# Attention weights transposed by the DMA crossbar instead of TensorE, with all v products moved into the attention stretch

## The chip, the cores and the metric

The kernel runs on one core of one Trainium2 chip. The metric is the device time of one execution in microseconds (us), less is better. Each run below is the median of its executions on one chip, beside executions of the kernel before on the same chip.

The kernel keeps its tiles in two memories: those that TensorE writes in pools of PSUM (`ps_1` and `ps_2` below), those of the pools `work` and `group` in SBUF. In the traces TensorE multiplies, VectorE, ScalarE and GpSimd do the rest of the arithmetic, and SyncE only issues DMAs, as GpSimd also does.

A second number goes through the whole text: the **period**. The kernel works on 128 batches in 32 groups of four, and in the middle each group repeats the one before. I take the start of the first TensorE product number 5 (the second q/k product) of each group from the trace, and average its distance from group to group over groups 2 to 29. One microsecond of period is about 31 us of the time.

## The reference, cut to what matters

```python
# layer 0: x is 128 batches of 128 x 512, fp32
x = layernorm(x + relu(max_over_the_512_columns(adj @ x) + b))
# layer 1: attention with 8 heads, masked by adj, then a projection and a norm
q, k, v = x @ w_qkv
attn = softmax(mask(q @ k.T * scale))          # 8 x 128 x 128 per batch
o = (attn @ v) @ w_proj + b_proj
x = layernorm(x + o + layernorm(o) * ln_gamma + ln_beta)
```

The attention product in both kernels reads `attn` transposed (`pav<-eT,v` in the traces, 2048 times for 128 batches), so the kernel needs eight transposed 128x128 blocks of fp32 per batch.

## The kernel before

Every engine works through a list of its own, in a fixed order that is set by "places" (numbers in a table, roughly microseconds after a TensorE step). An engine that waits at one entry of its list is late at the later ones, too. The dense products are done in split precision: each operand is split in a high, a low and a correction part (`h`, `l`, `d`), which VectorE and ScalarE prepare.

```python
work = ctx.enter_context(tc.tile_pool(name="work", bufs=2))
...
ps_1 = ctx.enter_context(tc.tile_pool(name="ps_1", bufs=4, space=bass.MemoryType.PSUM))
ps_2 = ctx.enter_context(tc.tile_pool(name="ps_2", bufs=2, space=bass.MemoryType.PSUM))
...
def transpose_e(b):                       # TensorE: eight transposes of a batch
    e, _ = es.pop(b)
    ppts[b] = ps_2.tile([P, H, P], FP, tag="ps2", name=f"ppt_{b}")
    for j in range(H):
        nc.tensor.transpose(ppts[b][:, j, :], e[:, j, :], ident)

def weights_T(b):                         # ScalarE: out of PSUM
    eTs[b] = work.tile([P, H, P], FP, tag="eT", bufs=2, name=f"eT_{b}")
    nc.scalar.copy(eTs[b], ppts.pop(b))
...
def residual_o(b):                        # GpSimd issues an accumulating DMA
    if b < B - G:
        nc.gpsimd.dma_start(xbs[b], os[b], accum_op=ALU.add)
...
def norm_1(b):                            # VectorE
    o, s, xb = os[b], sums_of.pop((b, 1)), xbs.pop(b)
    ...
    nc.vector.scalar_tensor_tensor(
        o, o, s[:, 2:3], gamma_sb, op0=ALU.add, op1=ALU.mult,
    )
    add_sum(b, 2, o, s[:, 1:2], xb)
...
# the order of TensorE in the attention stretch
'pair_order': [('T', 0), ('x', 1), ('T', 1), ('x', 0), ('S', 0), ('S', 1), ('AV', 0), ('AV', 1),
               ('dense', 2), ('po', 0), ('dense', 3), ('po', 1), ('T', 2), ('x', 3), ('T', 3), ('x', 2),
               ('S', 2), ('S', 3), ('AV', 2), ('AV', 3)],
```

In these lists `S` are the scores of a batch, `T` the transposes of its weights, `AV` the attention product, `x` the transposes of the layer-0 result, `conv` the graph product (tile `pa`), `dense` 0 to 3 the v products, `dense` 4 to 11 the q/k products, and `po` the projection.

## Time and profile before

| | before |
|---|---|
| time, median of 3 runs | 2041.28 us (2040.32 to 2041.9) |
| period | 61.92 us |
| TensorE idle between 60 and 2000 us | 12.8 us in all |
| VectorE, ScalarE busy | 81%, 71% |
| moved by DMA | 240.67 MB |

The table reads as follows. Of TensorE's 12.8 us of idle, 9.2 are two waits at the ends of the stretch; from 100 to 1980 us it is 3.6 us in all. So TensorE's own list is the length of a period. VectorE and ScalarE have 19% and 29% of their time free. The prediction shows the lines.

### The profile page before, as it was taken

What the parts mean: (1) busy time and instruction counts of PE and PEld (TensorE: products, weight loads), DVE (VectorE), ACT (ScalarE), POOL (GpSimd) and SP (SyncE); (2) the same over time, 40 slices, a digit from 0 to 9 for tenths busy, and PEclk for the clock granted to TensorE, in tenths of its full rate; (3) what the DMA queues carried; (4) which work ended last, traced back from release to release, by engine and by line L of the source; (5) the groups of instructions that cost most, each with busy time, mean ns of one, the idle gap of its engine ahead of it and who ended that gap; (6) DMA issues with size and microseconds to landing.
All of it is one profiled execution on the core that took longest, in us unless ns stands there. A gap on an engine that the chain in (4) does not pass through costs nothing. (4 is left out here: it accounts for less than half of the span.)

```text
span 2038.5 us, 35386 instructions
## 1 busy us (share of the span) xinstructions
PE 1995.0 (98%) x12033; PEld 1601.2 (79%) x12033; DVE 1652.2 (81%) x2615; ACT 1455.4 (71%) x4130; POOL 694.2 (34%) x1484
## 2 busy tenths in 40 slices
PE   7999999999999999999999999999999999999995
PEld 4688877888887888887888778888878887778874
DVE  7788777987778887778887779877788877798877
ACT  6676867776877767777768677667777677777665
POOL 1132434323334323343223343233343243432234
PEclk8999999999999999999999999999999999999998
DMA  4455455655455545555554545454455544455443
GB/s 151 88 119 119 118 125 106 130 114 129 115 119 110 130 120 124 120 111 123 121 123 115 127 106 130 112 130 117 117 112 128 121 121 123 106 124 124 104 104 88
DMA packets 134437, 240.67 MB, mean 118 GB/s; under 512 B 14704, under 2 KB 18928, under 8 KB 134256
## 3 DMA queue, kind: packets, MB, share of 16 engines
q1 hardware_dynamic: 97680, 172.27, 28.4%
q0 software_dynamic: 36288, 66.08, 22.1%
q8 instruction: 95, 1.56, 0.3%
q14 instruction: 86, 0.70, 0.1%
q10 hardware_dynamic: 288, 0.07, 0.0%
HBM read 138.74 MB, written 100.66 MB: 117 GB/s over the span
## 5 line engine op out<-in xcount | busy, mean ns | idle before, releaser
L333 ACT ACTIVATE e<-e,nmax 128x128 f32<-128x128 f32 x1024 | 396.8, 390 | 183.9 <-DVE nmax L326 183.9
L400 POOL DMA_DIRECT2D xb<-o x124 | 132.8, 1071 | 479.2 <-DVE o L405 449.3
L417 POOL TENSOR_SCALAR sum<-sum 128x1 f32<-128x1 f32 (+1 forms) x322 | 63.5, 197 | 433.5 <-ACT square L411 422.9
L418 POOL TENSOR_TENSOR sum<-sum,mhalf 128x1 f32<-128x1 f32 (+1 forms) x322 | 200.7, 623 | 26.8
L411 ACT ACTIVATE square<-o,sum 128x512 bf16<-128x512 f32 x256 | 183.2, 716 | 15.5 <-DVE o L405 13.1
L333 ACT ACTIVATION_READ_ACCUMULATOR e<-e,nmax 128x1 f32 x1024 | 192.4, 188 | 0.0
L423 POOL TENSOR_SCALAR sum<-sum 128x1 f32<-128x1 f32 x256 | 89.7, 350 | 281.4 <-DVE o L405 280.8
L432 DVE SCALAR_TENSOR_TENSOR o<-o,sum,gamma_sb 128x512 f32<-128x512 f32 x128 | 95.6, 747 | 88.7 <-DMA xb<-o 41.9
L342 DVE TENSOR_TENSOR e<-e,sums 128x1024 f32<-128x1024 f32 x128 | 156.8, 1225 | 4.4
L318 DVE SCALAR_TENSOR_TENSOR e<-psc,mask 128x1024 f32<-128x1024 f32 x128 | 155.5, 1216 | 2.3 <-PE psc L311 2.3
L326 DVE TENSOR_REDUCE nmax<-e 128x8 f32<-128x1024 f32 x128 | 155.2, 1212 | 0.1
L217 POOL DMA_DIRECT2D x<-in_L_gnn_ln_beta_dram x128 | 140.3, 1196 | 10.3 <-issue 10.3
L352 ACT COPY eT<-ppt 128x1024 f32<-128x1024 f32 x128 | 124.9, 1001 | 17.4 <-PE ppt L348 17.4
L348 PE MATMUL ppt<-ident,e 128*128 128x128 f32 x1024 | 132.3, 273 | 0.5 <-DVE qkT L300 0.5
L311 PE MATMUL psc<-qkT 64*128 64x128 f32 x2048 | 131.9, 279 | 0.0
L174 PE MATMUL pa<-xt,adjT 128*128 128x512 f32 x256 | 126.8, 619 | 5.1 <-DMA xt<-in_x_dram 4.7
L311 PEld LDWEIGHTS psc<-qkT 64*128 64x128 f32 x2048 | 119.4, 188 | 11.0 <-issue 5.5
L361 PE MATMUL pav<-eT,v 128*64 128x128 f32 x2048 | 126.4, 276 | 1.2 <-ACT eT L352 1.2
L348 PEld LDWEIGHTS ppt<-ident,e 128*128 128x128 f32 x1024 | 117.6, 141 | 9.5 <-DVE qkT L300 0.8
L190 ACT ACTIVATE xt<-xt,rm 128x512 f32<-128x512 f32 x128 | 91.4, 715 | 37.7 <-POOL rm L184 37.7
L361 PEld LDWEIGHTS pav<-eT,v 128*64 128x64 f32 x2048 | 110.4, 137 | 9.7 <-ACT eT L352 2.2
L440 ACT ACTIVATE o<-o,sum 128x512 f32<-128x512 f32 x128 | 103.0, 806 | 16.5 <-POOL sum L426 16.5
(4778 smaller groups left out, 5615.5 us busy)
## 6 DMA issues: line engine op xcount, KB each, us to landing
xt<-in_x_dram SPq DMA_DIRECT2D x128, 256.0 KB, 2.8
x<-xt SPq DMA_DIRECT2D x128, 256.0 KB, 2.1
x<-in_L_gnn_ln_beta_dram POOLq DMA_DIRECT2D x128, 256.0 KB, 8.6
xb<-x SPq DMA_DIRECT2D x128, 256.0 KB, 3.0
o<-in_L_gnn_b_proj_dram SPq DMA_DIRECT2D x128, 256.0 KB, 4.8
out_dram<-o SPq DMA_DIRECT2D x128, 256.0 KB, 2.0
xb<-o POOLq DMA_DIRECT2D x124, 256.0 KB, 4.2
wraw<-in_L_gnn_w_qkv_dram SPq DMA_DIRECT2D x12, 256.0 KB, 3.2
```

The source lines that it names most:

```text
L174: nc.tensor.matmul(pa[b], adjT, xs[b], start=True, stop=True)
L217: nc.gpsimd.dma_start(x1s[b], row(ln_beta), accum_op=ALU.add)
L311: nc.tensor.matmul(psc[:, s, hp, :], qkT[hs, hp, i, :], qkT[hs, KC + hp, i, :], start=True, stop=True,)
L318: nc.vector.scalar_tensor_tensor(e, pscs.pop(b).rearrange("p s a m -> p (s a) m"), scale, mask_b, op0=ALU.mult, op1=ALU.add,)
L326: nc.vector.tensor_reduce(nmax, es[b], AX.X, ALU.max, negate=True)
L333: nc.scalar.activation(e[:, j, :], e[:, j, :], AF.Exp, bias=nmax[:, j : j + 1], accum_out=sums[:, j : j + 1],)
L342: nc.vector.tensor_tensor(e, e, sums[:, :, None].to_broadcast([P, H, P]), op=ALU.mult)
L348: nc.tensor.transpose(ppts[b][:, j, :], e[:, j, :], ident)
L361: nc.tensor.matmul(pavs[b][s * HD : (s + 1) * HD, hp, :], v[:, h * HD : (h + 1) * HD], eT[:, s * HP + hp, :], start=True, stop=True,)
L400: nc.gpsimd.dma_start(xbs[b], os[b], accum_op=ALU.add)
L411: nc.scalar.activation(square, x, AF.Square, bias=s[:, 0:1], scale=-float(D), accum_out=s[:, 1:2],)
L418: nc.gpsimd.tensor_tensor(s, s, mhalf[:, :n], op=ALU.pow)
```

## The change

The intent is to relieve the engine that is full. ScalarE separates each fp32 weight into its two 16-bit halves, a DMA stores these two planes to DRAM, and a crossbar load (`DMA_TRANSPOSE` in the traces) brings them back transposed, half by half, so that the fp32 words stand together again. TensorE loses 8 transposes a batch. The bias of the projection becomes a constant in SBUF, which saves one load a batch; `o` and `v` have fewer buffers than before (3 instead of 4, 4 instead of 6). All places were set anew, and all four v products moved into the attention stretch, with two of the four projections and two of the four graph products.

```diff
+    def halves(b):
+        e, _ = es.pop(b)
+        planes = work.tile([P, 2, H * P], U16, tag="planes", bufs=1, name=f"planes_{b}")
+        nc.scalar.copy(
+            planes, e.rearrange("p h m -> p (h m)").bitcast(U16).rearrange("p (m s) -> p s m", s=2),
+        )
+        rows[b] = dram.tile([P, 2, H * P], U16, tag="rows", bufs=8, name=f"rows_{b}")
+        nc.sync.dma_start(rows[b], planes)
+
+    def crossbar_T(b):
+        eTs[b] = work.tile([P, H, P], FP, tag="eT", bufs=2, name=f"eT_{b}")
+        nc.sync.dma_start_transpose(
+            eTs[b].rearrange("p h n -> p (h n)").bitcast(U16).rearrange("p (h r) -> p h r", h=H),
+            rows.pop(b).rearrange("n s m -> (n s) m"),
+        )
...
-                vs[g, j] = group.tile([P, D], FP, tag="v", bufs=6, name=f"v_{g}_{j}")
+                vs[g, j] = group.tile([P, D], FP, tag="v", bufs=4, name=f"v_{g}_{j}")
...
-            os[b], pps["o", b][0], 1.0 + 1.0 / HALF, os[b], op0=ALU.mult, op1=ALU.add,
+            os[b], pps["o", b][0], 1.0 + 1.0 / HALF, bias_sb, op0=ALU.mult, op1=ALU.add,
...
-         'beta': [25.0, 24.85, 24.59, 24.66],
+ 'beta': [4.57, 2.09, 14.96, 45.33],
...
+ 'pair_order': [('S', 0), ('S', 1), ('AV', 0), ('AV', 1), ('dense', 0), ('po', 0), ('dense', 1),
+                ('po', 1), ('S', 2), ('AV', 2), ('x', 0), ('S', 3), ('AV', 3), ('x', 1),
+                ('dense', 2), ('dense', 3), ('x', 2), ('x', 3), ('conv', 0), ('po', 2), ('conv', 1),
+                ('po', 3)],
...
+ 'softmax': {'cross': [-14.48, -14.68, -13.71, -6.73],
...
+             'halves': [5.82, 2.29, 0.68, 4.53],
```

The row `beta` sets when GpSimd issues the accumulating DMAs that add `ln_beta` to the stored layer-0 rows.

## The prediction

> **What bounds the kernel now.** I read the page's busy shares first, then the slices, then one repeating stretch of the middle by windows, then the order of time on TensorE and VectorE inside it. The page's list of waits comes last, since it only means something once the bound is known.
>
> ```profile
> span 2038.5 us, 35386 instructions
> ## 1 busy us (share of the span) xinstructions
> PE 1995.0 (98%) x12033; PEld 1601.2 (79%) x12033; DVE 1652.2 (81%) x2615; ACT 1455.4 (71%) x4130; POOL 694.2 (34%) x1484
> ...
> PE   7999999999999999999999999999999999999995
> ...
> PEclk8999999999999999999999999999999999999998
> ```
>
> TensorE is full in all slices but the ends, at full granted clock. The busy share by itself would not prove it (matmuls overlap in the record), so I looked at two windows of 62 us:
>
> ```profile
> core 0: us, PE busy (x) PEld busy (x) DVE busy (x) ACT busy (x) POOL busy (x), PEclk, DMA share, GB/s
> ...
> 738.00:800.00 62.00, 62.00 (x378) 49.90 (x377) 50.73 (x81) 45.04 (x129) 21.53 (x46) 1.00 0.52 119
> 800.00:862.00 62.00, 62.00 (x378) 49.93 (x377) 50.73 (x81) 45.05 (x130) 21.54 (x46) 1.00 0.53 120
> ```
>
> No microsecond without a matmul in flight, VectorE at 50.7 and ScalarE at 45.0 of 62. So the middle is a queue of TensorE work, and a group of four batches costs what its TensorE work costs. The order of time on TensorE gives the period and the slots:
>
> ```profile
> 745.00 1.04 PE L348 MATMUL ppt<-ident,e 128*128 128x128 f32 x8
> 745.87 0.60 PE L224 MATMUL ptx<-ident,xt 128*128 128x128 f32 x4
> ...
> 751.60 1.99 PE L174 MATMUL pa<-xt,adjT 128*128 128x512 f32 x4
> 753.01 0.80 PE L261 MATMUL pp_('o', 42)_7670<-p_h,oh 128*128 128x512 f32 x1
> 753.65 0.39 PE L262 MATMUL pp_('o', 42)_7670<-p_l,ol 128*128 128x512 f32 x1
> ...
> 806.88 1.04 PE L348 MATMUL ppt<-ident,e 128*128 128x128 f32 x8
> ```
>
> Columns: start, length, engine, line, operation. The same place one group later is 806.88 - 745.00 = 61.88 us on, the period. Eight transposes of the attention weights of one batch hold the engine from 745.00 to 745.87: a slot of 0.87 us. The graph product pa is followed by a product whose first matmul holds the engine for 0.64 us (753.01 to 753.65) where its neighbours take about 0.23: leaving pa for a product costs 0.4 us, and before pays it twice a group, since the four pa come in pairs.
>
> [...] This trace has 273 ns from start to end, but eight of them start 109 ns apart (0.87/8), so the slot counts, not the latency. [...] One of the new transfers is 256 x 1024 halves of 2 bytes, 512 KB[...]. Nothing in the trace before decides that, as it has no such transfer. [...]
>
> **The change, part by part.** For 124 of 128 batches:
>
> *Removed from TensorE*: 8 transposes, 0.87 us a batch, 3.48 a group. Over the 31 groups it applies to that is 108 us, the most it can give: 2041 - 108 = 1933.
>
> *Added to TensorE*: the new order separates the four pa from each other (conv 0, projection 2, conv 1, projection 3; conv 2, product 7, conv 3). Four switches instead of two: +0.8 us a group. And all four v products move out of the dense stretch into the attention stretch, so the scores of the next group come directly behind the last q/k product. The last two of their eight head products wait for the VectorE addition to that q/k tile. In the trace before, the addition to v starts 0.27 us after the next TensorE work (789.26 against 788.99) and takes 0.69, so the wait ends about 1.0 us after the product; the first six heads cover 0.75 of it. +0.27 us a group.
>
> *ScalarE*: the copy of the transposed weights out of PSUM goes (1001 ns for 1024 columns), and the copy that separates the halves comes, over 2048 elements a partition. From 616 ns (512 columns) to 1001 (1024) it is 0.75 ns a column, so 1001 + 1024 x 0.75 = 1.77 us, some 0.8 us more than before: +3.1 a group, 45.0 becomes 48.1 of about 60, or 80%. Not the bound.
>
> *VectorE*: the same instructions, 50.7 us in a group that now is about 60 instead of 62; 85%. It is uneven, and that matters: in the attention stretch the new order puts before the head split of the last batch (starts to starts in the trace: 1.14 masking, 1.13 row maximum, 1.37 weights, 0.60 for 512-wide additions and differences, 1.33 for the first two steps of a split, 1.40 for a projection's pair, 1.53 for a first norm) 3 maskings, 2 maxima, 2 weights, 8 splits, 6 differences, 2 projections, 4 v additions, 1 norm: 3.42 + 2.26 + 2.74 + 10.64 + 3.60 + 2.80 + 2.40 + 1.53 = 29.4 us. It starts when the first scores are out (1.5 us) and I count 1.2 us of waits for TensorE in it, so the split is there at about 32.1. TensorE's own work to that point: 4 scores 4.0 (two take 1.98), 4 attention products 3.8, 4 x transposes 1.9, 7 products of 2.80, pa twice with one switch 1.8, the 0.27 above and 0.2 for small switches: 31.6. So about 0.5 us of TensorE idle a group, in front of the fourth projection.
>
> *DMA*: a 512 KB store and a 512 KB crossbar load more each batch, a 256 KB bias load less. The hardware queue moved 172.27 MB at 28.4% of the span, so about 300 GB/s when busy: 1.75 us for the store[...], 0.9 less for the bias, per 15 us: share 0.52 becomes 0.7. The weights of a group are stored a whole stretch before they are used; only the third and fourth crossbar loads wait for a buffer of two, free after the first two attention products. The fourth comes in the SyncE order behind the output store of the previous group's last batch, which I place at 10.5 us after the scores, with its use at 18.8: 8 us of room. A streaming crossbar[...] is hidden; the change's own placing keeps at least 3 us.
>
> *Sum*: 61.88 - 3.48 + 0.8 + 0.27 + 0.5 = 60.0 us a group, 1.9 saved, times 31 = 59: 2041 - 59 = 1982. The tail and start change little (the last four batches still transpose on TensorE). I take 1980.
>
> **Rivals.** (1) *The order fits better than my count*: no wait at the fourth projection and for the scores, 59.2 a group, 1958. For it: all the places were set anew, surely to shut such gaps. Against: the VectorE sum above has almost no slack. (2) *VectorE becomes the bound of the attention stretch*, with 1 to 2 us more than I count, because norms wait for accumulating DMAs as they do now:
>
> ```profile
> L432 DVE SCALAR_TENSOR_TENSOR o<-o,sum,gamma_sb 128x512 f32<-128x512 f32 x128 | 95.6, 747 | 88.7 <-DMA xb<-o 41.9
> ...
> xb<-o POOLq DMA_DIRECT2D x124, 256.0 KB, 4.2
> ```
>
> That idle costs nothing today, as VectorE catches up in the dense stretch. With one norm in the middle of the attention stretch and busier DMA engines it would go straight to TensorE: 61 to 62 a group, 2010 to 2040, the same. (3) *The crossbar goes block by block*[...]: the fourth attention product waits[...] in each group, and SyncE, which issues in order, holds up loads behind it: 2100 to 2350. Against: [...]the short distances chosen. (4) *The single buffer of the halves holds up ScalarE*: the second copy must wait for the 512 KB store of the first (256 KB stores land in 2.0 to 2.1 us, so 3 to 4). I count about 2 us of ScalarE idle there once a group, and 1 to 2 us of room before the v addition behind it feels it. If it did not fit, another 0.5 to 1 us a group: about 2000.
>
> **Range and chances.** 1980, with rival 1 as the good end (1940 if the ends gain too) and rival 2 as the bad one (2030). The 2% line is 2000.5, only 0.65 us a group away from my count, hence 0.68 faster; 0.25 same; 0.07 slower for the crossbar.
>
> **What would show it.** The period in the order of time: 60.0, with the transposes gone and ScalarE's copy of halves at about 1.8 us. TensorE idle, or stretched first matmuls, at the scores (0.3) and at the fourth projection (0.5), released by VectorE or by ScalarE's cast behind it. VectorE over 83% busy. The crossbar load landing in under 8 us and no idle of the attention products for it. Wrong would be: attention products waiting for a DMA (rival 3), VectorE waiting for the accumulated residual within the attention stretch (rival 2), or a period below 59.2, which would mean that the switch of pa or the waits are cheaper than they look here.

The 273 ns are those of one transpose, from the trace before; what that trace does not decide is how long a crossbar load takes. The sum came to 60.0 us a group and 1980 us, in which the crossbar load has no term because it was taken to be hidden. The DMA share of 0.7 counts a time for the load (the store and the bias alone make it 0.58: 0.85 us more in 15). That "a streaming crossbar", one without pauses between its blocks, is hidden, and the 2100 to 2350 us of rival 3, were assumptions and not shown.

## The result, and the profile after

| | before | after |
|---|---|---|
| time, median of 4 runs beside each other | 2041.59 us | 2157.08 us (2149.46 to 2161.51) |
| ratio | | 1.0562 (1.0531 to 1.0594) |
| period | 61.92 us | 65.71 us |
| TensorE idle, 60 to 2000 us | 12.8 us | 151.6 us |
| TensorE below full clock, 60 to 2000 us | 11.9 us | 133 us |

The changed kernel is right and 5.6% slower. The last row adds up the records of a granted clock below full speed.

The head of the page of the changed kernel, with TensorE's busy share and its slices:

```profile
span 2159.7 us, 33692 instructions
...
PE 1967.0 (91%) x11041; PEld 1528.7 (71%) x11041; DVE 1665.0 (77%) x2615; ACT 1548.3 (72%) x4130; POOL 694.7 (32%) x1484
...
PE   7889999889999999989999999999999999899996
```

TensorE has 992 instructions fewer, and is no longer full. The same two windows that the prediction read say it more sharply:

```profile
core 0: us, PE busy (x) PEld busy (x) DVE busy (x) ACT busy (x) POOL busy (x), PEclk, DMA share, GB/s
738.00:800.00 62.00, 59.04 (x325) 46.20 (x325) 47.74 (x75) 44.82 (x124) 20.25 (x44) 0.97 0.73 160
800.00:862.00 62.00, 58.55 (x313) 45.46 (x312) 48.46 (x77) 44.73 (x121) 22.67 (x46) 0.97 0.71 165
```

Where it was 62.00 of 62 us, TensorE is now busy 59, its clock is granted at 0.97, VectorE does less per microsecond and not more, and the DMA share went from 0.52 to 0.73. The list of waits (engine, line, what ended the wait; us in total, times, longest) names them:

```profile
ACT planes L351 <- DMA rows<-planes: 146.9, 30, 9.1
...
PE pav L382 <- DMA eT<-rows: 94.4, 32, 5.5
...
DVE o L450 <- DMA xb<-o: 47.3, 45, 6.2
```

Once a group the attention product waits for its crossbar load, once a group ScalarE waits for the store of the planes before it may fill their only buffer again, and VectorE waits for the accumulated residual. The list of DMA issues (size, median us from issue to landing) puts the store at 3.2 us and the crossbar load at 6.1:

```profile
rows<-planes SPq DMA_DIRECT2D x124, 512.0 KB, 3.2
...
eT<-rows SPq DMA_TRANSPOSE x124, 6.1
```

The first three crossbar loads of a group keep SyncE for 2.6, 2.2 and 2.6 us in the median, the fourth for 7.7. One such place in the order of time, first on TensorE (start, length, engine, line, operation; in brackets the idle time before it and what ended it):

```profile
930.56 1.16 PE L314 MATMUL psc<-qkT 64*128 64x128 f32 x16
936.65 1.97 PE L382 MATMUL pav<-eT,v 128*64 128x128 f32 x16 [4.93 <-DMA eT<-rows]
938.55 1.12 PE L227 MATMUL ptx<-ident,xt 128*128 128x128 f32 x4
```

The same place on SyncE and on GpSimd:

```profile
917.16 2.41 SPq L360 DMA_TRANSPOSE eT<-rows  x1
...
924.52 8.55 SPq L360 DMA_TRANSPOSE eT<-rows  x1
```

```profile
918.68 1.81 POOL L220 DMA_DIRECT2D x<-in_L_gnn_ln_beta_dram  x2 [9.15 <-DMA x<-xt]
920.67 0.81 POOL L220 DMA_DIRECT2D x<-in_L_gnn_ln_beta_dram  x1 [0.18 <-issue]
```

GpSimd issues three `ln_beta` loads at 918.68 to 921.5, since two of them waited for a store and came out together with the next. They are accumulating DMAs: from 922 to 928 the 16 DMA engines are nearly full of their packets, and the last ends at 931.8 (40 to 74 begin each microsecond, 284 to 391 ns each in the mean). The fourth crossbar load is issued at 924.52, in the midst of it; the trace has no packet of it before 928. Most of its packets of 929 to 932 take 18 ns as usual, but a few take up to 3.9 us, so that the mean of a microsecond is 58 to 194 ns. Its last packet ends at 934.6, 10.1 us after the issue, where the packets of two loads of the same size in a quiet stretch, from 906.1 to 910.5, needed 4.5 us together. It is not alone in this: between 922.1 and 926.9 SyncE's queue moves no data at all, and the output store and the residual load that SyncE issued just before, at 922.55 and 923.06, land after 10.0 and 10.1 us, where 2.7 and 2.9 are the medians. And the wait has a second price, which the windows show (same columns as above):

```profile
934.00:936.00 2.00, 0.00 (x0) 0.00 (x0) 1.74 (x3) 0.00 (x0) 1.21 (x2) 0.66 1.08 326
936.00:940.00 4.00, 3.35 (x22) 2.92 (x23) 0.24 (x1) 0.00 (x0) 0.00 (x0) 0.50 0.97 261
940.00:942.00 2.00, 2.00 (x7) 1.59 (x6) 1.85 (x4) 1.70 (x1) 0.00 (x0) 0.64 0.45 137
```

During these 4.93 us without work TensorE's clock is halved (the record begins at 934.6) and stays so until about 941: the attention product has a slot of 1.90 us (936.65 to 938.55) and not 0.95. In this trace half clock goes with waits, but no one length of a wait decides it. From 60 to 2000 us the changed kernel has 26 records of half clock, each with one wait of 1.9 us or more; nine of these waits are shorter than 3 us (1.93 to 2.96). Four waits of 1.6 to 1.8 us and one of 3.42 us cost no clock. The profile page's digits of the clock in its slices still read 9 all through the middle, so the loss has to be looked for in narrow windows.

The loss can be written as a sum. The period before was 61.92; without the transposes 58.44; +0.8 for two more switches of pa, as predicted, and +0.26 for the scores, as measured (a pair takes 2.24 us instead of 1.98): 59.5. In the stretch of 60 to 2000 us there are 29.5 periods of after and 31.3 of before. Idle: 151.6/29.5 - 12.8/31.3 = 4.7. Half clock loses half of its time (1.90 us for the slot of 0.95 above), and only what does not lie in the idle already counted: 109.5 of the 133 us, and 9.1 of the 11.9 before, so (109.5/29.5 - 9.1/31.3)/2 = 1.7. Together 65.9 against a measured 65.7; so the parts are good to some tenths, and nothing large is missing.

### The profile page after: what moved, and what is told of

Its sections match the earlier page's. It is cut to its first block, busy times and chain, and to the rows that moved or that the text cites. A ratio compares the mean times of both kernels' runs of the same rounds, so it can differ in the third digit from the quotient of the medians.

```text
span 2159.7 us, 33692 instructions
## 1 busy us (share of the span) xinstructions
PE 1967.0 (91%) x11041; PEld 1528.7 (71%) x11041; DVE 1665.0 (77%) x2615; ACT 1548.3 (72%) x4130; POOL 694.7 (32%) x1484
## 5 line engine op out<-in xcount | busy, mean ns | idle before, releaser
L351 ACT COPY planes<-e 128x2048 uint16<-128x2048 uint16 x124 | 234.7, 1892 | 152.7 <-DMA rows<-planes 146.9
L382 PE MATMUL pav<-eT,v 128*64 128x128 f32 x2048 | 147.4, 296 | 97.0 <-DMA eT<-rows 94.4
L220 POOL DMA_DIRECT2D x<-in_L_gnn_ln_beta_dram x128 | 113.7, 988 | 322.0 <-DMA x<-xt 309.0
L382 PEld LDWEIGHTS pav<-eT,v 128*64 128x64 f32 x2048 | 121.3, 147 | 111.2 <-DMA eT<-rows 94.2
L441 POOL TENSOR_SCALAR sum<-sum 128x1 f32<-128x1 f32 x256 | 129.7, 507 | 213.0 <-DVE o L423 213.0
L177 PE MATMUL pa<-xt,adjT 128*128 128x512 f32 x256 | 137.7, 625 | 30.1 <-issue 28.1
L235 DVE TENSOR_SCALAR xh<-ptx 128x512 int32<-128x512 int32 x128 | 87.7, 685 | 97.7 <-PE ptx L227 97.3
L329 DVE TENSOR_REDUCE nmax<-e 128x8 f32<-128x1024 f32 x128 | 155.1, 1211 | 0.1
L314 PE MATMUL psc<-qkT 64*128 64x128 f32 x2048 | 148.9, 286 | 0.0
L227 PE MATMUL ptx<-ident,xt 128*128 128x128 f32 x512 | 89.7, 313 | 25.3 <-ACT xt L212 16.8
L423 DVE SCALAR_TENSOR_TENSOR o<-o,sum,xb 128x512 f32<-128x512 f32 x128 | 96.2, 752 | 15.0 <-POOL sum L436 0.9
```

Of the source, the lines that this page charges most:

```text
L177: nc.tensor.matmul(pa[b], adjT, xs[b], start=True, stop=True)
L314: nc.tensor.matmul(psc[:, s, hp, :], qkT[hs, hp, i, :], qkT[hs, KC + hp, i, :], start=True, stop=True,)
L329: nc.vector.tensor_reduce(nmax, es[b], AX.X, ALU.max, negate=True)
L351: nc.scalar.copy(planes, e.rearrange("p h m -> p (h m)").bitcast(U16).rearrange("p (m s) -> p s m", s=2),)
L382: nc.tensor.matmul(pavs[b][s * HD : (s + 1) * HD, hp, :], v[:, h * HD : (h + 1) * HD], eT[:, s * HP + hp, :], start=True, stop=True,)
L441: nc.gpsimd.tensor_scalar(s[:, 2:3], s[:, 0:1], -1.0 / D, None, op0=ALU.mult)
```

## The experiments

At first I held **theory A**: the fourth crossbar load meets the three `ln_beta` loads, and this one wait with its half clock is the loss. The rival, **theory B**: the new order has several chains of almost equal length, and to free one only lets the next come out.

### The collision, two ways

Issue the fourth crossbar load earlier, right behind the third:

```diff
- 'softmax': {'cross': [-14.48, -14.68, -13.71, -6.73],
+ 'softmax': {'cross': [-14.48, -14.68, -13.71, -14.5],
```

This run, and the ones further down that move the second copy of planes, also hold each load behind the store of its own planes, so that it cannot come before it.

> Only the fourth crossbar load of each group moves: in the SyncE order it stands directly behind the third instead of behind the output store and the residual load. Theory A (the load waits in the DMA engines behind three accumulating loads of ln_beta, the idle of TensorE of 2.9 us a group is that wait, and the half clock that follows an idle costs about 2 us more): issue of the fourth load falls from 7.7 us to 2 to 3 us, the attention product no longer waits, half clock after the start is nearly gone, the period falls from 65.7 to 60 to 61 us, the time to 1980 to 2015 us. Rival B (VectorE is the bound of the new attention stretch and the wait for the load only hides it): the idle moves to another instruction, period 63 or more, time above 2075.

Measured: 2169.29 us, ratio 1.0624 (1.0596 to 1.0652), period 65.84. The fourth load still keeps SyncE 7.5 us in the median: third and fourth now go out together, the `ln_beta` loads come out at the same time, and they collide as before. The run missed its aim and decides nothing.

Put the `ln_beta` loads back to the places that they had before:

```diff
- 'beta': [4.57, 2.09, 14.96, 45.33],
+ 'beta': [25.0, 24.85, 24.59, 24.66],
```

> Only the four places of the accumulating loads of ln_beta go back to those of the kernel before, 25 us behind the norm, which takes them away from the fourth crossbar load. Theory A (collision with the accumulating loads): the fourth crossbar load is issued in under 3.5 us and lands in under 7, wait of the attention product under 0.5 us a group, time 1985 to 2020 us. Rival C (the fourth load is late because of its place in the SyncE order, whatever else is in flight): its issue begins at the same place, 12 us after the scores, it lands after 17 to 18 with the use at 18, so no large change from this run would be left to C only if its landing stays at 10 us or more: then time above 2120.

Measured: 2175.65 us, ratio 1.0654 (1.0638 to 1.067), period 66.57. The collision is gone completely: the fourth load keeps SyncE 2.3 us from the same place in its order (so the place alone, rival C of the expectation, was not the cause), there is no idle at all in front of attention products from 60 to 2000 us, and the time below full clock falls from 133 to 68 us. Yet the kernel is not faster. The waits of this run:

```profile
DVE o L450 <- DMA xb<-o: 112.2, 77, 3.8
ACT planes L351 <- DMA rows<-planes: 111.5, 29, 6.4
...
PEld ptx L227 <- ACT v L299: 63.4, 30, 3.4
```

And two lines of its order of time show how one wait becomes another on the way to TensorE:

```profile
1062.37 1.90 ACT L351 COPY planes<-e 128x2048 uint16<-128x2048 uint16 x1 [3.72 <-DMA rows<-planes]
```

```profile
1066.52 0.65 PE L227 MATMUL ptx<-ident,xt 128*128 128x128 f32 x4 [1.83 <-ACT v L299]
```

ScalarE stands 3.72 us in front of its second copy of planes; the copy of a v product stands behind it in ScalarE's list, and the transposes on TensorE need the PSUM buffer that this copy frees. A second chain is longer still. TensorE's largest wait in this run is at the first q/k product of a group, for VectorE's `x_d`: 74.8 us in 28 places from 60 to 2000 us, against 12.3 in the changed kernel. In 27 of the 28 VectorE had stood, less than 6 us earlier, at a norm that waited for its accumulated residual; the `ln_beta` loads are now in flight beside 90 of the 124 accumulating DMAs of the residual (31 in the changed kernel), and these land after 6.7 us in the median beside them, after 3.4 without. One such place:

```profile
1012.88 0.75 DVE L450 SCALAR_TENSOR_TENSOR o<-o,sum,gamma_sb 128x512 f32<-128x512 f32 x1 [2.02 <-DMA xb<-o]
...
1015.16 1.19 PE L272 MATMUL pp_(15, 4)_9309<-x_d,w_d 128*128 128x512 f32 x4 [1.94 <-DVE x_d L241]
```

So the collision is real, but theory A as the one cause has fallen.

Move the fourth attention product to a later place on TensorE, so that it has more room:

```diff
-                ('po', 1), ('S', 2), ('AV', 2), ('x', 0), ('S', 3), ('AV', 3), ('x', 1),
-                ('dense', 2), ('dense', 3), ('x', 2), ('x', 3), ('conv', 0), ('po', 2), ('conv', 1),
+                ('po', 1), ('S', 2), ('AV', 2), ('x', 0), ('S', 3), ('x', 1),
+                ('dense', 2), ('AV', 3), ('dense', 3), ('x', 2), ('x', 3), ('conv', 0), ('po', 2), ('conv', 1),
```

> The fourth attention product is moved behind the third v product on TensorE (2.8 us of useful work before the wait), its load and its head split keep their places in the other orders. The load still lands 10 us or more after its issue, so the wait falls from 2.9 us a group to about 0.5. If an idle[...] costs half clock afterwards (theory A), that cost of about 2 us a group goes too: gain 4 to 4.5 us a group, time 2015 to 2050. If the clock cost were not a result of the idle: gain 2.4 us a group, time 2075 to 2095. Rival B (VectorE bound): gain under 1 us a group, above 2120, as the head split behind this product comes later.

Measured: 2132.33 us, ratio 1.044 (1.0404 to 1.0475), period 64.65. Idle at attention products falls from 90 to 13 us, but idle in front of the x transposes, which wait for ScalarE's v copies, rises from 17 to 68 us. This is the pattern of theory B again: 77 us freed, 51 of them given back in the next place.

### How much is the order, how much the traffic

Four runs take out parts of the traffic; all give wrong results. First, all of it: ScalarE still copies the planes, but they are neither stored nor loaded, and the attention product reads a constant.

```diff
-        nc.sync.dma_start(rows[b], planes)
...
-        nc.sync.dma_start_transpose(...)
+        eTs[b] = eT_fixed
```

> Wrong result on purpose: the halves are copied by ScalarE as in the changed kernel but neither stored nor loaded back; the attention products read one constant tile. All other work keeps its order and places. If the loss is all DMA traffic and the waits for it (theory D), what is left is the count of the prediction: period 59.5 to 61, no half clock, time 1970 to 2010. If the new order itself is worse than counted, with VectorE and ScalarE late in the attention stretch whatever the transfers do (rival B): period 63 or more, time above 2075.

Measured: 2040.54 us (2 runs), ratio 0.9996 (0.9976 to 1.0016), period 61.58. This was the most telling run: **with the transposes gone from TensorE and no traffic at all in their place, the new order is just as long as the old one.** The 3.48 us a group that were taken off TensorE are lost within the order itself. The largest loss, 49.5 us in 29 places (1.7 us each), is in front of the first pa:

```profile
1129.26 1.04 PE L227 MATMUL ptx<-ident,xt 128*128 128x128 f32 x8
1132.24 2.02 PE L177 MATMUL pa<-xt,adjT 128*128 128x512 f32 x2 [1.94 <-issue]
```

```profile
1131.45 0.69 DVE L237 TENSOR_TENSOR x_l<-ptx,xh 128x512 fp32r<-128x512 f32 x1
```

The releaser is given as "issue", which says that the profile saw no semaphore for it. The time tells: VectorE's last reading of an x transpose ends at 1132.14, and pa starts at 1132.24; in all 29 places the distance is 0.10 us. These tiles share the four PSUM buffers of `ps_1`, so pa waits for VectorE to empty one.

Then the store alone (the load replaced by the constant):

> Wrong result on purpose: the 512 KB stores run, the crossbar loads do not (constant tile instead). Theory D with two separate holders: the second copy of halves still waits for the store of the first through the one buffer, shorter since SyncE is not held by a crossbar issue (2 to 3 us instead of 4.7 a group), and costs TensorE 1 to 2 us a group: period 61 to 62.5, time 2010 to 2060. If the stores are harmless: as without traffic. If the stores are the larger part: above 2090.

Measured: 2079.38 us (2 runs), ratio 1.0186 (1.0149 to 1.0222), period 63.12.

The load alone (the first eight batches' planes are read again and again, nothing stored later):

> Wrong result on purpose: only the first eight batches store their halves, later crossbar loads read those eight again, so the loads run with nothing to wait for but their buffer. The accumulating loads of ln_beta are where the change put them. Theory D: the fourth load is still issued in 7 to 8 us behind them and the attention product still waits about 3 us a group with half clock after it: period 63.5 to 65, time 2080 to 2130. If the stores or the wait of the copies cause most of the loss: under 2040.

Measured: 2190.94 us (2 runs), ratio 1.0732 (1.0702 to 1.0762), period 66.37, with 78 us idle at attention products: no better than the whole change. So most of the price is the load's, and the two prices do not add up: 1.5 and 4.8 us a group over the 61.6 without traffic, where both together cost 4.1.

An ordinary load of the same bytes in runs of 4 KB, and an ordinary copy of the planes, instead of crossbar and splitting:

```diff
-        nc.sync.dma_start_transpose(
-            eTs[b].rearrange("p h n -> p (h n)").bitcast(U16).rearrange("p (h r) -> p h r", h=H),
-            rows.pop(b).rearrange("n s m -> (n s) m"),
+        nc.sync.dma_start(
+            eTs[b].rearrange("p h n -> p (h n)").bitcast(U16),
+            rows.pop(b).rearrange("n s m -> n (s m)"),
```

> Wrong result on purpose: the weights are stored unsplit (the ScalarE copy keeps its 2048 elements) and the 512 KB come back by a plain load of 4 KB runs in place of the crossbar load, so not transposed. Same places, same bytes, same waits. If only the bytes queued behind the accumulating loads count: the fourth load is as late (10 us) and the time stays within 2130 to 2170. If the form of the crossbar load counts (2048 packets of 256 B, SyncE held for the whole issue[...]): the plain load lands in 5 to 6 us, the wait mostly goes, time 2000 to 2060.

Measured: 2105.93 us, ratio 1.03 (1.0273 to 1.0326), period 63.78. About half of the traffic's price (4.1 us) goes with the crossbar, but an ordinary load waits at the same place, 57 us in 29 attention products, and the fourth of a group lands after 9.2 us in the median (10.8 with the crossbar; ScalarE's copy takes 1.89 us as before). So the collision does not need the crossbar, which makes it longer.

### What the order could have gained

The order of before, its TensorE transposes left out, and ScalarE copying the untransposed weights (wrong):

```diff
     def transpose_e(b):
+        if b < B - G:
+            return
```

> Wrong result on purpose: the kernel before, in its own order, without the TensorE transposes of 124 batches; ScalarE copies the weights untransposed from where they lie, so that the dependence weights, copy, attention product stays. It shows what the removal alone is worth in the old order. If TensorE is the only bound there (the step of the prediction that took 0.87 us a batch off): period 58.4 to 59, time 1930 to 1955. If VectorE or the PSUM slots already stand close behind in the old order: 59.5 to 61, time 1970 to 2020. The difference between this and the run of the new order without traffic (2040) is what the new order itself costs.

Measured: 2006.73 us, ratio 0.9837 (0.982 to 0.9853), period 60.89. So even the tuned old order turns 3.48 us less TensorE work into only 1.0 us less time. The rest shows as idle in one place per group and as small stretches of other slots:

```profile
1045.77 0.50 PE L261 MATMUL pp_('o', 62)_10299<-p_h,oh 128*128 128x512 f32 x1 [0.79 <-ACT oh L248]
```

A projection waits for ScalarE's cast of the attention result. That cast follows VectorE's split of it, so the chain comes from VectorE's list.

Was VectorE the bound of the new order, too? Without traffic, four of its 512-wide steps a group (the correction part of the attention result) left out, 2.4 us a group:

```diff
     def split_d(key):
+        if isinstance(key, tuple) and key[1] < B - 2 * G:
+            return
```

> Wrong result on purpose: the new order without store and load of the halves, and VectorE leaves out the last step of the four splits of the attention outputs (0.6 us each, all in the attention stretch and ahead of the instructions that TensorE waited for). If the attention stretch of the new order is bound by VectorE's queue (theory V): TensorE's idle in front of the first graph product, 1.6 us a group, goes; period 59.4 to 60.3, time 1965 to 2005. If not VectorE but another wait sets it: less than 0.5 us a group, above 2025.

Measured: 2020.46 us (2 runs), ratio 0.9906 (0.9886 to 0.9926), period 60.85. VectorE's list is on the path, but 2.4 us less of it gave 0.7; the PSUM wait at pa is still 37 us.

Without traffic, the third projection moved ahead of the two pa, which gives VectorE time to empty the buffer:

```diff
-                ('dense', 2), ('dense', 3), ('x', 2), ('x', 3), ('conv', 0), ('po', 2), ('conv', 1),
+                ('dense', 2), ('dense', 3), ('x', 2), ('x', 3), ('po', 2), ('conv', 0), ('conv', 1),
```

> Wrong result on purpose: as the run without store and load, but TensorE does the third projection before the two graph products of the attention stretch instead of between them (their other places kept). That run had a period of 61.6 where the prediction counted 60.0, and TensorE idle 1.4 to 1.9 us in front of the first graph product in each group, ending just as VectorE finished reading the third x transpose. If the PSUM slot that this transpose holds is the term that the count left out: the idle goes and with it one of the switches of 0.4 us, period 59.3 to 60.3, time 1965 to 2005. If VectorE's work itself was the limit, the idle comes back at another instruction: period 61 or more, above 2020.

Measured: 2053.93 us (2 runs), ratio 1.0064 (1.0033 to 1.0094), period 62.28. The idle at pa is gone, and 39 us of idle stand now in front of a q/k product that waits for VectorE's `x_d`. Same pattern.

### Mending one chain after the other

Three runs build on each other, all with right results. First, the later `ln_beta` places and ScalarE's second copy of planes later, where its buffer is free:

```diff
-             'halves': [5.82, 2.29, 0.68, 4.53],
+             'halves': [5.82, 13.6, 0.68, 4.53],
```

> The accumulating loads back at the places of the kernel before (as in the run that did this alone, which removed the wait for the fourth crossbar load completely but gained nothing), and the second copy of halves moved behind the casts and the v copies on ScalarE, so that its wait for the buffer holds up nothing. In the run before, TensorE then waited 1.8 us a group for a v copy on ScalarE, 1.3 for a cast, and 3.2 for VectorE that stood at a norm waiting for an accumulated residual. Theory D: the first two go, the third stays or shrinks: period 62 to 64, time 2040 to 2105. If it gains less than 1 us a group (time above 2135), the single buffer was not what held ScalarE's chain.

Measured: 2122.6 us, ratio 1.0397 (1.038 to 1.0414), period 64.61: 53 us less than with the later `ln_beta` places alone. Idle at attention products and x transposes is gone. What is left stands at the q/k product that waits for `x_d` (67 us, where it was 75) and at pa (46 us, where it was 2). Next, the projection ahead of the two pa (the edit above), and an earlier place for that `x_d`. This run is called the third mended order below, the later `ln_beta` places alone being the first:

```diff
- 'x_d': [3.55, 4.38, 6.93, 0.57],
+ 'x_d': [3.55, 4.38, 1.6, 0.57],
```

> On top of the run with the accumulating loads and the second copy of halves moved (period 64.6): the same move of the third projection ahead of the graph products, and the last step of the third x split on VectorE ahead of the norm that waits for an accumulated residual. In that run TensorE idled 1.5 us a group at the graph product and 2.3 at the first q/k product, released by this last step, and ran at half clock for 3.1 us a group afterwards. If these two waits are what is left of the loss: period 59.5 to 61.5, half clock nearly gone, time 1970 to 2030, the first version under the kernel before. If another chain of nearly the same length takes over (theory of many equal chains): period 62 to 64, above 2040.

Measured: 2117.8 us, ratio 1.0375 (1.036 to 1.0391), period 64.23. The half clock is back at 13.7 us (11.9 before the change); the one large DMA wait left on VectorE in this run is the norm that needs the accumulated residual:

```profile
DVE o L450 <- DMA xb<-o: 136.6, 61, 5.5
```

That is 4.4 us a group. Next, the norm of the second batch of each group, with its statistics and output, moved 3 to 4 us later to let the residual land:

> As the run before, and the norm of the second batch, which waits for the accumulated residual, goes 4 us later on VectorE, with its statistics and its output. If VectorE's wait there still costs after the last step of the split was moved ahead of it: 0.3 to 1 us a group better than the run before. If it does not: equal within 0.5%.

Measured: 2250.5 us, ratio 1.103 (1.1012 to 1.1049), period 68.62. It holds the `xb` buffer longer, so the next residual is loaded later: GpSimd waits 253.6 us in this run for those loads to land, where it waited 41.5 in the run before. A clear miss. The residual cannot be given time by moving its user; it has to be ready sooner. The test of that leaves the accumulating DMA out of the third mended order. Its output is wrong, which doesn't matter for the time.

> Wrong result on purpose: the third of the mended kernels (stores and crossbar loads run, period 64.2, no half clock left), without the accumulating DMA that adds the projection to the residual; the norm reads the residual as loaded. If what the traffic still costs there is VectorE standing at norms for this accumulation (4.4 us of such waits a group): period 61.5 to 62.5, as the same order without traffic, time 2035 to 2065. If the crossbar and store traffic costs by another way: period stays above 63.5, time above 2095.

Measured: 2007.03 us (2 runs), ratio 0.984 (0.982 to 0.986), period 60.68. All the 3.6 us a group that the third mended order had above this are the accumulated residual: VectorE standing for it, its traffic, or the time in which GpSimd issues it. The run does not part these three. As with the later `ln_beta` places alone, 90 of the 124 residuals of the third mended order are in flight beside `ln_beta` loads (6.7 us to landing, 3.4 without); a third place for those loads was not tried.

### The residual by GpSimd instead of an accumulating DMA

GpSimd spends 1.05 us on issuing that DMA anyway. The next three runs let it do the addition itself, with a right result:

```diff
-            nc.gpsimd.dma_start(xbs[b], os[b], accum_op=ALU.add)
+            nc.gpsimd.tensor_tensor(xbs[b], xbs[b], os[b], op=ALU.add)
```

In the third mended order:

> The third mended order, with the accumulating DMA of the residual (GpSimd issues it, it takes 4.6 us and more to land, 256 KB of read and write) replaced by an addition on GpSimd itself. The result stays right. If VectorE's standing for the accumulated residual is what the crossbar's traffic still costs (run without residual: 2007 us, period 60.6), this lands near it: 2005 to 2035 us, VectorE's wait before the last norm under 0.5 us a batch, and it beats the kernel before (2041). If GpSimd's addition is slow (over 3 us) or holds VectorE up[...], VectorE's durations grow and the time stays at 2060 to 2120 us.

Measured: 2037.67 us, ratio 0.9993 (0.9978 to 1.0007), period 61.66: 80 us better than the third mended order, and even with the kernel before. In the kernel before:

> The kernel before with the same addition on GpSimd in place of the accumulating DMA. There the residual was waited for little, TensorE idles 12.8 us in all, so: 2030 to 2045 us, same. If GpSimd's addition slows VectorE, slower than 2045 us. This says how much of the gain of the run beside it belongs to the crossbar change, and how much to the residual's way alone.

Measured: 2097.67 us, ratio 1.0285 (1.0269 to 1.03), period 63.98: there the same edit costs 58 us. In the changed kernel:

> The changed kernel with only the residual's way changed: the fourth crossbar load still meets the three ln_beta loads, so its wait of some 3 us and the half clock stay: 2110 to 2150 us. If it drops under 2080 us, the accumulating residual, not the ln_beta loads, is what delays the fourth crossbar load.

Measured: 2142.0 us, ratio 1.0493 (1.047 to 1.0515), period 65.53, the fourth crossbar load still 7.7 us long. So the gain is not the edit's own: it comes only where the residual is the chain that is left.

Why did it cost 58 us in the old order? Two places of the third mended order with this edit show it, first on VectorE, then on GpSimd:

```profile
1008.58 1.56 DVE L241 SCALAR_TENSOR_TENSOR x_d<-x_l,xh 128x512 fp32r<-128x512 f32 x1
...
1019.85 1.21 DVE L321 SCALAR_TENSOR_TENSOR e<-psc,mask 128x1024 f32<-128x1024 f32 x1
...
1021.58 2.32 DVE L450 SCALAR_TENSOR_TENSOR o<-o,sum,gamma_sb 128x512 f32<-128x512 f32 x1
```

```profile
1008.31 1.28 POOL L418 TENSOR_TENSOR xb<-xb,o 128x512 f32<-128x512 f32 x1
...
1019.83 1.30 POOL L418 TENSOR_TENSOR xb<-xb,o 128x512 f32<-128x512 f32 x1 [0.93 <-DMA xb<-x]
...
1021.76 1.58 POOL L418 TENSOR_TENSOR xb<-xb,o 128x512 f32<-128x512 f32 x1
```

The first VectorE step takes 1.56 us instead of 0.68 and ends 0.55 us after GpSimd's addition; the last takes 2.32 instead of 0.75 and ends 0.56 us after it. The middle one, which reads one operand from PSUM, takes its usual 1.21. So beside an addition on GpSimd the two steps with two SBUF inputs stretched, and the one with an input from PSUM did not; by what mechanism, the trace does not show. In the kernel before, the edit stretched three kinds of VectorE steps, all with two SBUF inputs, in the mean over all of them: from 1225 to 1455 ns, 752 to 996 and 683 to 1003 (the masking, which reads PSUM, stayed at 1216 and 1213 ns, the row maximum, which reads one operand, at 1212 and 1211). The stretching is 0.79 us a batch or 3.2 a group, where the period grew by 2.1.

So the last run moves two of the four additions of a group beside steps that read PSUM or one operand:

```diff
-            'residual_o': [11.11, 15.58, 7.45, 8.03],
+            'residual_o': [11.11, 3.2, 7.45, 2.8],
```

> The third mended order with the residual added on GpSimd, and two of the four additions of a group moved so that each runs beside VectorE steps that read PSUM or one operand. In the run before, VectorE's step x_d took 1.56 instead of 0.68 us beside an addition of GpSimd (both operands in SBUF) and a norm's step 2.32 instead of 0.75; masked, row maximum and the steps from PSUM did not stretch. TensorE's one large gap of a group, 1.15 us at a projection waiting for VectorE's ol, came behind that stretched x_d. If the stretch causes it: period 61.66 - 1.15 = 60.5 us, 1995 to 2015 us, ratio 0.98 to 0.99, faster than both kernels with a right result; mean of x_d back under 0.75 us and of the norm's first step under 0.85. If the stretch is no matter, or the idle comes back at another in-order slot as in the earlier mended orders: 2030 to 2045 us.

Measured: 2016.01 us (2015.26 to 2017.41), ratio 0.9881 (0.9864 to 0.9897), period 60.95, with a right result. In its groups by line (busy us, mean ns, idle before) both steps have their old lengths:

```profile
L450 DVE SCALAR_TENSOR_TENSOR o<-o,sum,gamma_sb 128x512 f32<-128x512 f32 x128 | 96.3, 752 | 32.7 <-POOL sum L441 31.1 <-POOL xb L418 1.0
...
L241 DVE SCALAR_TENSOR_TENSOR x_d<-x_l,xh 128x512 fp32r<-128x512 f32 x128 | 87.9, 687 | 1.2
```

And its page:

```profile
span 2014.5 us, 33394 instructions
...
PE   7889999999999999999999999999999999999996
```

This version beats the changed kernel by 141 us and the kernel before by 25 us, 1.2%. That is a real difference by its interval, but less than 2%.

## Why the prediction was wrong

The prediction said 1980 us, 0.68 for faster; 2157 us was measured, slower. In periods that is 65.7 us instead of 60.0. The run without traffic (61.6) parts the 5.7 us: 1.6 belong to the order itself, 4.1 to the transfers that were thought hidden. Point by point:

**Removed from TensorE, 3.48 us a group.** The instructions went as counted, from 12033 to 11041. That they are worth 3.48 us is the first step that failed. "The middle is a queue of TensorE work" was true, but it says only that TensorE was the longest chain, not by how much. The run of the old order without transposes measured the lead of TensorE over the next chain: 1.0 us a group, not 3.5 (its places were not set anew, so it is a measure of that order and no limit). Three further runs (no traffic and less VectorE work; third mended order without residual; the last version) stop at 60.85, 60.68 and 60.95 by quite different ways. None reached the predicted 60.0.

**Two more switches of pa, and the scores.** The scores' pair came at 2.24 us, +0.26 against a predicted 0.27. The switches are as counted: 117 products behind a pa from 60 to 2000 us (60 before) hold the engine for 0.63 us with their first matmul, where neighbours take 0.23.

**VectorE 0.5 us late at the fourth projection.** The sum of VectorE's steps was of the right kind, and its place was wrong. In the run without traffic TensorE loses 1.7 us, not 0.5, in front of the first pa, at a PSUM buffer that VectorE has not yet emptied. The prediction followed who needs VectorE's results, not who needs the buffers that it reads.

**ScalarE's copy of halves.** Predicted 1.77 us, measured 1.89. Its single buffer (rival 4) was counted at 2 us idle once a group; it was 146.9 us in 30 places, 4.9 each, and with the `ln_beta` loads moved it reached TensorE by way of the v copy. The median of 3.2 us for the stores mixes four places of a group. The one that this wait is for, the group's first, lands after 4.7 us in the median, and SyncE issues it 1.2 us after ScalarE's copy has ended, with crossbar loads in front of it in its list. That makes the wait; with the `ln_beta` loads moved the 1.2 us go to 0.03, and 3.7 us of wait are left.

**DMA: the fourth crossbar load "is hidden".** This is the step that failed hardest: the 4.1 us of traffic begin with it. The rate was not the trouble: two loads in the quiet stretch went through in 4.5 us from first packet to last, 2.2 each. The landing of the fourth was assumed, from no trace, as if it ran alone, within 8 us of room. It met three accumulating loads whose places the change had moved into this very stretch; in the example it landed after 12.1 us (10.1 to its last packet), and in the median after 10.8, where the first two of a group take 5.2 and 4.7. The row `beta` stood in the diff, and the prediction did not work out where it would put those loads. Rival 3 expected such a wait for another cause, a slow crossbar, and that cause is out: with the `ln_beta` loads elsewhere all four loads of a group land after 4.5 to 5.7 us in the median (what the form of the load costs is the 1.9 us a group that the ordinary load saved). Nor was the wait the whole miss: that run, without it, is no faster.

**What no line of the prediction had** is the half clock. It cost TensorE another 1.7 us a group. The kernel before shows it twice, outside its middle: the waits of 4.71 us at 69.4 and of 4.49 at 1992.4 are each followed by 6.8 us of half clock.

**Rival 2** (norms waiting for the accumulated residual) was put down as the bad end, 61 to 62 us. It is what was left once the other chains had been mended, and at 3.6 us a group (with its traffic and its issue) it was larger than thought.

What stays open: how the 2.5 us a group between the ideal and what the best runs reach divide between VectorE's list, ScalarE's casts and PSUM. The runs show that each takes part, and that idle moves when one is shortened; they do not give one number for each. Nor was it tried whether the kernel before gains from additions on GpSimd when they are well placed; so the 1.2% of the last version cannot be put down to the crossbar. Whether two buffers for the planes would help was not tried either.

## What to carry to other kernels

A full engine tells that its list is the longest chain, not how far the next is behind; leave the work out (with a wrong result, on purpose) and time that before building a substitute for it. When a change gives a new transfer a place, look at what the other queues issue in the same microseconds, accumulating DMAs first (here the fourth crossbar load landed after 10.8 us beside them, after 4.5 to 5.7 without), and remember that a wait can cost TensorE half its clock on top (here 26 waits of 1.9 us and more did, one of 3.42 us did not). In a schedule of fixed lists mend the chains one after the other and look after each which came out next: here that turned 5.6% slower into 1.2% faster.
